# Layer 0 of a four-layer image kernel: all position evictions on VectorE, two images ahead of the other two, and the output maxima spread over the steps

## The chip, the cores and the metric

The kernel runs on one core of one Trainium2 chip. The core has five engines that work side by side, each through its own queue in order: TensorE for matrix products (PE in the profile, with its weight loads shown as PEld), VectorE (DVE), ScalarE (ACT), GpSimd (POOL) and SyncE (SP), which here only issues transfers. They meet through semaphores. Matrix products are written to PSUM, eight banks of 512 float32 columns on 128 partitions; everything else lies in SBUF or in the memory outside the core.

The metric is the device time of one execution in microseconds (us). Lower is better.

## The reference

The input is a float32 tensor of 4 images, 16 channels and 512 x 512 pixels. Four layers follow one another. The change touches the first alone:

```python
pos = conv_general_dilated(x, pos_w, padding=1, feature_group_count=16)   # 3x3 taps, each channel for itself
x = x + pos + pos_b
y = affine(x)                                # per pixel, 16 -> 16 channels
win = windows of 8 x 8 pixels of y           # 64 tokens of 16 channels
q, k, v = win @ qkv_w.T + qkv_b              # 2 heads of 8 channels
attn = softmax(q @ k.T / sqrt(8))            # 64 x 64 in each window and head
x = x + (attn @ v) @ proj_w.T + proj_b
x = x + gelu(affine2(x) @ fc1_w.T + fc1_b) @ fc2_w.T + fc2_b
```

Layer 1 begins with a fake quantisation, for which the largest absolute value of all of layer 0's output must be known: `alpha = max(|x|)`. After it come a 3 x 3 convolution with a batch norm and a clip, a pair of 3 x 3 convolutions with a residual, and a 3 x 3 convolution with a pixelwise MLP.

## The kernel before, in words

Layer 0 is written in `window_attention`. It works in 64 steps. A step n takes a block of 8 rows and 64 columns in eight strips of each of the four images: the 128 partitions hold 4 pairs of strips (V, index `vv`) of 2 x 16 channels, and the images are the index `u`. The loop `for n in range(STEPS)` holds three steps in flight at a time: step n is finished, the keys and queries of step n+1 are made, and the taps of step n+2 are summed.

PSUM is shared out by hand. Banks 0 and 1 are the tile `pair0`, banks 2 and 3 `pair1`; banks 4 to 7 are single. The taps of image u (`depthwise`, L287, nine of them, 32 x 32 matmuls, four for each tap) sum up in bank u. `position` (L302 on VectorE for images 0 and 1, L298 on ScalarE for images 2 and 3) adds the bias and writes them to `y`, in the order of windows. The same four banks later take the scores.

The order on each engine is the order of the program text; nothing reorders it, since the engines stand under `tc.manual_schedule`. A step runs like this:

1. `values(0)` (L338) turns the first values round into bank 4; VectorE copies them out (L346). `scores(0)` (L353) fills banks 0 to 3, four windows of four images; ScalarE takes exponentials of one pair of banks at a time (L361). Then `output` of the step before (L432, L437) adds the second MLP product to the residual, into the tile `xo`.
2. For k = 1 to 7: `scores(k)`, `values(k)` (copied out by ScalarE, at k = 7 by VectorE), `attend(k-1)` (L374), and `divide(k-1)`: two transposes (L389) and a reciprocal (L394) on VectorE, a product on GpSimd (L396), and later `turn_back` (L403) on VectorE. SP issues stores and key turns (L90, L310) here. Each turn ends with one `highest_output()` (L452), which takes the largest absolute value of one piece of `xo`, if the list `largest` holds any.
3. `attend(7)`, the last `divide` and `turn_back`, then 16 blocks of queries and taps, `highest(n + 1)` (L329) on VectorE, one more `highest_output()`, and `project` (L409) with its residual sums (L414).
4. A tail of 44 blocks in an order written as a string. A `d` is one tap of one image; an `h` is one product of the MLP's first layer (`hidden`, L421) with its gelu on ScalarE (L426); a `q` is a query product (L319), copied out by VectorE (L326). Block i works in rows `32 * (i % 4)` of the array, so four blocks that follow one another use different rows. The `h` and `q` blocks take banks 6, 7, 4, 5 in turn.

The tile `xo` covers two steps. Only after the second of them, `store` puts its pieces on the lists `stores` and `largest`, eight maxima of 4 rows by 128 columns. So they are taken in every second step, one at each call of `highest_output()`; these are called even steps below (n even), and the others odd.

In the last step there are no taps and queries, and each image's output is made and sent inside the tail.

Of the kernel before, what the change touches and what calls it, by code (L numbers as in the profile page):

```python
# [12 lines left out]
F32 = mybir.dt.float32  # L13
BF16 = mybir.dt.bfloat16
AF = mybir.ActivationFunctionType
ALU = mybir.AluOpType
# [9 lines left out]
P = 128  # L26
# [5 lines left out]
WS = 8  # L32
# [54 lines left out]
def _store_block(nc, x1, src, b, r0, cols, queues=None):  # L87

    rows = x1.rearrange("m (r c) b x -> (m r) c b x", r=2)[r0 + 1 : r0 + 1 + WS, :, b, cols]
    (next(queues) if queues else nc.sync).dma_start(rows.rearrange("m c x -> c m x"), src)  # L90
# [53 lines left out]
def window_attention(ctx: ExitStack, tc, xw, x1, hots, m, v, peak):  # L144
# [14 lines left out]
    nc = tc.nc  # L159
    U = V = 4  # L160
    BW = 64
    NJ = BW // WS
    N = NJ * T
# [11 lines left out]
    def bank(i):  # L175
        return pairs[i // 2][:, i % 2, :] if i < 4 else singles[i - 4]

    def quad(i):
        return slice(32 * i, 32 * i + 32)
# [3 lines left out]
    def load(k):  # L183
        t = xin.tile([P, V, WS + 2, BW + 2], F32, tag="x", name=f"x{k}")
        nc.sync.dma_start(t, xw[k])
        return t

    xts, ys = {0: load(0), 1: load(1)}, {}
# [72 lines left out]
    px = ctx.enter_context(tc.tile_pool(name="w0x", bufs=2))  # L261
# [15 lines left out]
    def by_window(ap):  # L277
        return ap.rearrange("p (j a x) -> p a j x", a=WS, x=WS)

    def by_row(ap):  # L280
        return ap.rearrange("p (a j x) -> p a j x", a=WS, x=WS)

    def depthwise(n, tap, u):

        dy, dx = divmod(tap, 3)
        for vv in range(V):
            nc.tensor.matmul(  # L287
                bank(u)[quad(vv)], taps[quad(u), tap, :],
                xts[n][quad(u), vv, dy : dy + WS, dx : dx + BW],
                start=tap == 0, stop=tap == 8,  # L290
            )

    def position(n):

        y = px.tile([P, U, N], F32, tag="y", name=f"y{n}", bufs=3)
        for u in range(U):
            if u // 2:
                nc.scalar.activation(  # L298
                    by_window(y[:, u]), by_row(bank(u)), AF.Identity, bias=v("pos_b")
                )  # L300
            else:
                nc.vector.tensor_scalar(  # L302
                    by_window(y[:, u]), by_row(bank(u)), v("pos_b"), None, ALU.add
                )
        return y

    def turn_keys(y, vv):
        for u in range(U):
# [39 lines left out]
    def scores(k, n):  # L348

        vv, jl = k // 2, 4 * (k % 2)  # L350
        for i, jj in ((0, 0), (0, 1), (1, 0), (0, 2), (1, 1), (0, 3), (1, 2), (1, 3)):
            for u in (2 * i, 2 * i + 1):
                nc.tensor.matmul(  # L353
                    bank(u)[:, P * jj : P * jj + P],
                    y2[quad(u), vv, jl + jj].rearrange("p w t -> p (w t)"),
                    g[quad(u), vv, jl + jj].rearrange("p h t -> p (h t)"),
                    start=True, stop=True,
                )
        e = px.tile([P, U, 4, P], F32, tag="e", name=f"e{n}_{k}", bufs=3)
        for i in range(2):  # L360
            nc.scalar.activation(  # L361
                e[:, 2 * i : 2 * i + 2].rearrange("p u j t -> p u (j t)"),
                pairs[i], AF.Exp,
            )
        return e
# [52 lines left out]
    def hidden(y, u, vv, b, n):  # L418

        for k in range(4):  # L420
            nc.tensor.matmul(  # L421
                b[quad(k)], fc1[quad(vv), quad(k)], y[quad(vv), u, :],
                start=True, stop=True,
            )
        hd = px.tile([P, N], F32, tag="hid", name=f"hid{n}_{u}_{vv}", bufs=16)
        nc.scalar.activation(hd, b, AF.Gelu, bias=f1b)  # L426
        return vv, hd

    def output(y, xo, hids, us, banks, n):

        for k, (vv, hd) in enumerate(hids):
            nc.tensor.matmul(  # L432
                bank(banks[k // 4])[quad(vv)], m("fc2"), hd, start=True, stop=True
            )
        at = BW * (n % 2)
        for u, i in zip(us, banks):
            nc.vector.tensor_tensor(  # L437
                xo[:, u, :, at : at + BW].rearrange("p a (j x) -> p a j x", x=WS),
                by_window(bank(i)), by_window(y[:, u]), ALU.add,
            )  # L440
        if n % 2:
            store(xo, n // 2, us)


    queues = itertools.cycle((nc.sync, nc.gpsimd))

    stores, largest = [], []

    def highest_output(k=1):
        for _ in range(min(k, len(largest))):  # L450
            xo, i = largest.pop(0)
            nc.vector.tensor_reduce(  # L452
                peak[:, i : i + 1], xo, AX.XY, ALU.max, apply_absolute_value=True
            )

    def store(xo, k, us):
        i, cb = divmod(k, NQ)
        for u in us:
            for a in range(2):
                half = slice(WS // 2 * a, WS // 2 * a + WS // 2)  # L460
                largest.append((xo[:, u, half], 2 * (U * k + u) + a))
            for strip in range(2 * V):
                stores.append((xo[C * strip : C * strip + C, u], u, SR * strip + WS * i, cb))

    def send(k, queues=None):
        for _ in range(min(k, len(stores))):
            src, u, r, cb = stores.pop(0)
            _store_block(nc, x1, src, u, r, slice(XW * cb, XW * cb + XW), queues)
# [26 lines left out]
    for n in range(2):  # L495
        for tap in range(9):
            for u in range(U):
                depthwise(n, tap, u)
        xts[n + 2] = load(n + 2)
        ys[n] = position(n)  # L500
    highest(0)
    for vv in range(V):
        turn_keys(ys[0], vv)
# [3 lines left out]
    last, xo = None, None  # L507
    nc.scalar.preload_act_table_set("natural_log_exp_and_others")
    for n in range(STEPS):
        more, ahead = n + 1 < STEPS, n + 2 < STEPS  # L510
        taken, asked = [0] * U, [0] * V

        def block(what, i, b, scalar=False):
            at = i % 4
            if what == "q" and more:
                query(ys[n + 1], asked[at], at, b, scalar)
                asked[at] += 1
            elif what == "d" and ahead:
                depthwise(n + 2, taken[at], at)
                taken[at] += 1  # L520
                if taken == [9] * U:
                    ys[n + 2] = position(n + 2)

        values(0)
        es, ts = {0: scores(0, n)}, {}
        if last:

            output(*last)
        for k in range(1, 8):
            es[k] = scores(k, n)  # L530
            values(k)
            attend(es[k - 1], k - 1)
            ts[k - 1] = divide(k - 1, n, nc.gpsimd)
            if 1 < k < 7:
                turn_back(ts[k - 2], k - 2)
            if k == 1:
                send(8 * U)
            if k % 2 and more:
                turn_keys(ys[n + 1], k // 2)
            highest_output()  # L540
        nc.scalar.preload_act_table_set("gelu_and_others")
        attend(es[7], 7)
        ts[7] = divide(7, n, nc.gpsimd)
        for k in (5, 6, 7):
            turn_back(ts[k], k)
        free = iter((4, 5, 6, 7, 4, 5))
        for i, what in enumerate("qqddddqqqqdddddd"):
            block(what, i, bank(next(free)) if what == "q" else None, True)
        if more:
            highest(n + 1)  # L550
        highest_output()
        y = ys.pop(n)
        project(y)
        if n % 2 == 0:
            xo = px.tile([P, U, WS, XW], F32, tag="xo", name=f"xo{n}", bufs=1)
        if not more:
            flag = bounded()

        hids, units = [], itertools.cycle((6, 7, 4, 5))
        for i, what in enumerate("ddddhdhddhqhddhqhddhdhddhdhddhdhdhddhdddddhh"):
            if what == "h":
                q = len(hids)
                hids.append(hidden(y, q // 4, i % 4, bank(next(units)), n))
                if not more and q in (5, 9, 13):
                    u = q // 4 - 1
                    output(y, xo, hids[q - 5 : q - 1], (u,), (u,), n)
                    send(8, queues)
            else:  # L570
                block(what, i, bank(next(units)) if what == "q" else None)
        if n + 4 < STEPS:
            xts[n + 4] = load(n + 4)
        if more:
            nc.scalar.preload_act_table_set("natural_log_exp_and_others")
        last = (y, xo, hids, range(U), (5, 4, 6, 7), n)
    output(y, xo, hids[12:], (3,), (3,), n)
    send(8, queues)
    highest_output(2 * U)
    return nc.values_load(flag[0:1, 0:1], min_val=0, max_val=1)  # L580

# [792 lines left out]
```

## Time and profile before

| | |
|---|---|
| median of 3 runs | 5686.06 us (5681.55 to 5701.97) |
| the profiled execution | 5693.38 us |
| its span, first to last instruction | 5691.6 us |
| mean granted TensorE clock | 0.99 |
| layer 0's 64 steps, first transposes to the end of the loop | about 70 to 3189 us |
| busy in the span: PE, DVE, ACT, POOL | 5428.8, 3738.1, 3482.3, 707.5 us |
| L302 position, VectorE, x128 | 746 ns each |
| L298 position, ScalarE, x128 | 697 ns each |
| L452 maxima, VectorE, x256 | 640 ns each |

The rows of groups in the profile give a line of the code, the engine, the operation, what it writes and reads, how often it runs, its busy time, and the idle time of its engine just before it with what ended that. An engine's idle time matters only where the bottleneck waits for it. A timeline row gives start, duration, engine, line, operation, operands and count; in brackets stands the idle time before it and the releaser. In a list of waits a row gives who waited for whom, the total, how many times, and the longest.

### The profile page before, as it was taken

How to read it: one execution, taken by the hardware profiler on the slowest of the kernel's cores; microseconds unless marked ns; L12 is line 12 of the kernel's file. 1: busy time of each engine (PE TensorE's matmuls, PEld its weight loads, DVE VectorE, ACT ScalarE, POOL GpSimd, SP SyncE). 2: the span in 40 equal slices, each digit the busy share in tenths (PEclk: the TensorE clock that was granted, in tenths of full speed). 3: DMA queues.
4: the chain of work that ended last, by engine and by line, in shares of the span. 5: the costliest groups of instructions: out<-in, count | busy, mean ns of one | idle time of the engine just before them, and what ended most of it. 6: DMA issues, size and time to landing. Idle time of an engine off the chain costs nothing. (4 is left out here: it accounts for less than half of the span.)

```text
span 5691.6 us, 268539 instructions
## 1 busy us (share of the span) xinstructions
PE 5428.8 (95%) x120912; PEld 2891.5 (51%) x120912; DVE 3738.1 (66%) x5806; ACT 3482.3 (61%) x4739; POOL 707.5 (12%) x692
## 2 busy tenths in 40 slices
PE   7999999999999999999999765999999999999999
PEld 5666666666666666666676332322222222222222
DVE  4666666666666666666666555667676767676766
ACT  3777777777777777777777453444444444444444
POOL 1111111111111111111111352000000000000000
PEclk9999999999999999999999898999999999999999
DMA  2333333233333333333323697777767776777674
GB/s 79 77 75 74 77 71 77 65 82 71 80 73 78 73 79 73 74 77 72 81 65 60 140 247 182 173 174 176 175 174 177 174 176 173 177 175 177 173 177 107
DMA packets 626194, 677.47 MB, mean 119 GB/s; under 512 B 355856, under 2 KB 485008, under 8 KB 616848
## 3 DMA queue, kind: packets, MB, share of 16 engines
q1 hardware_dynamic: 624240, 658.76, 48.2%
q8 instruction: 953, 15.61, 1.2%
q14 instruction: 201, 1.65, 0.1%
q0 software_dynamic: 512, 1.05, 0.1%
q10 hardware_dynamic: 288, 0.39, 0.0%
HBM read 222.45 MB, written 134.48 MB: 63 GB/s over the span
## 5 line engine op out<-in xcount | busy, mean ns | idle before, releaser
L361 ACT ACTIVATE e<-pair 128x1024 f32<-128x1024 f32 x1024 | 992.8, 1022 | 449.0 <-PE pair L353 448.1
L287 PE MATMUL pair<-x,taps 32*32 32x512 f32 x18432 | 1073.8, 601 | 3.5 <-issue 2.2
L1206 ACT ACTIVATE hid<-tb,vec 128x512 f32<-128x512 f32 x1024 | 646.8, 684 | 630.7 <-PE tb L1198 630.7
L389 DVE STREAM_TRANSPOSE a<-bank 128x512 f32<-128x512 f32 x1024 | 669.9, 692 | 368.8 <-PE bank L374 354.6
L396 POOL TENSOR_TENSOR t<-a,r 128x512 f32<-128x512 f32 x512 | 542.1, 1059 | 2607.2 <-DVE r L394 2607.2
L426 ACT ACTIVATE hid<-bank,f1b 128x512 f32<-128x512 f32 x1024 | 641.4, 689 | 297.3 <-PE bank L421 233.1
L353 PE MATMUL pair<-g,y 32*128 32x128 f32 x16384 | 727.4, 287 | 50.2 <-DVE y L302 45.2
L1208 DVE TENSOR_SCALAR hid<-tb,vec 128x512 f32<-128x512 f32 x1024 | 717.9, 743 | 27.1 <-PE tb L1198 26.8
L353 PEld LDWEIGHTS pair<-g,y 32*128 32x128 f32 x16384 | 626.2, 186 | 198.1 <-issue 131.8
L421 PE MATMUL bank<-y,fc_e 32*32 32x512 f32 x8192 | 709.2, 606 | 1.0 <-DVE y L414 1.0
L374 PE MATMUL bank<-e,yt 64*32 64x128 f32 x32768 | 608.2, 274 | 28.1 <-DVE yt L346 21.0
L287 PEld LDWEIGHTS pair<-x,taps 32*32 32x32 f32 x18432 | 502.0, 103 | 182.2 <-issue 67.9
L1198 PE MATMUL tb<-ye,mat 32*128 32x512 f32 x4096 | 586.1, 639 | 0.0
L374 PEld LDWEIGHTS bank<-e,yt 64*32 64x32 f32 x32768 | 463.3, 106 | 128.3 <-issue 105.0
L1218 PE MATMUL tb<-hid,mat 128*32 128x512 f32 x4096 | 466.0, 595 | 0.0
L1123 PE MATMUL tb<-zo,cw 64*32 64x512 f32 x3096 | 365.7, 598 | 16.1 <-issue 8.9
L1123 PE MATMUL tb<-xo,cw 64*32 64x512 f32 x3096 | 361.5, 594 | 7.2 <-issue 5.3
L302 DVE TENSOR_SCALAR y<-pair,vec 128x512 f32<-128x512 f32 x128 | 90.2, 746 | 413.2 <-PE pair L287 413.2
L1123 PE MATMUL tb<-ho,cw 64*32 64x512 f32 x3072 | 357.4, 592 | 3.8 <-issue 3.0
L1123 PE MATMUL tb<-ze,cw 64*32 64x512 f32 x3072 | 360.8, 598 | 0.0
L1123 PE MATMUL tb<-he,cw 64*32 64x512 f32 x3072 | 357.7, 592 | 0.0
L1123 PE MATMUL tb<-xe,cw 64*32 64x512 f32 x3072 | 357.0, 594 | 0.0
(180 smaller groups left out, 7044.3 us busy)
## 6 DMA issues: line engine op xcount, KB each, us to landing
x<-in_xw_dram SPq DMA_DIRECT2D x64, 1320.0 KB, 5.8
zo<-ze SPq DMA_DIRECT2D x512, 128.5 KB, 2.4
ho<-he SPq DMA_DIRECT2D x512, 128.5 KB, 2.4
xo<-xe SPq DMA_DIRECT2D x512, 128.5 KB, 2.4
y<-y SPq DMA_DIRECT2D x2048, 32.0 KB, 2.6
tx<-x SPq DMA_DIRECT2D x256, 256.0 KB, 4.1
out_dram<-xe SPq DMA_DIRECT2D x128, 512.0 KB, 4.6
x<-xo SPq DMA_DIRECT2D x1008, 64.0 KB, 2.6
```

What stands on the lines that cost most here:

```text
L287: nc.tensor.matmul(bank(u)[quad(vv)], taps[quad(u), tap, :], xts[n][quad(u), vv, dy : dy + WS, dx : dx + BW], start=tap == 0, stop=tap == 8,)
L353: nc.tensor.matmul(bank(u)[:, P * jj : P * jj + P], y2[quad(u), vv, jl + jj].rearrange("p w t -> p (w t)"), g[quad(u), vv, jl + jj].rearra ...
L361: nc.scalar.activation(e[:, 2 * i : 2 * i + 2].rearrange("p u j t -> p u (j t)"), pairs[i], AF.Exp,)
L374: nc.tensor.matmul(bank(4 + 2 * (k % 2) + w)[quad(u), P * jj : P * jj + P], t[half, U * jj + u, w : w + 2].rearrange("p d c -> p (d c)"), ...
L389: nc.vector.transpose(a[:, 512 * w : 512 * w + 512], bank(4 + 2 * (k % 2) + w))
L396: engine.tensor_tensor(t.rearrange("p b w c -> p w b c"), top, r.unsqueeze(3).to_broadcast([P, 2, 16, C]), ALU.mult,)
L421: nc.tensor.matmul(b[quad(k)], fc1[quad(vv), quad(k)], y[quad(vv), u, :], start=True, stop=True,)
L426: nc.scalar.activation(hd, b, AF.Gelu, bias=f1b)
L1123: nc.tensor.matmul(p[r][_quad(2 * f + w)], weights[_half(r), odd, dx, :], src[_half(r), f, dx : dx + W], start=dx == 0, stop=dx == 2,)
L1198: nc.tensor.matmul(p[q], w1[_quad(q), 1 - par, :], inner(src)[_quad(q), f, :], start=True, stop=True,)
L1206: nc.scalar.activation(hd, p[q], AF.Relu, bias=v("l3_b1"))
L1208: nc.vector.tensor_scalar(hd, p[q], v("l3_b1"), 0.0, ALU.add, ALU.max)
```

## The change

All four images' positions are now written by VectorE. `position(n, i)` does one pair of images, and is called as soon as the nine taps of that pair are in: images 2 and 3 (`pair1`) come first, then 0 and 1. `scores` goes through the pairs in the other order, `pair1` first, and its exponentials too. The string of the tail is another one: the taps of images 2 and 3 are complete at places 34 and 35 (counted from 0), those of images 0 and 1 at 40 and 41 as before; two query blocks stand side by side; and `h` blocks no longer run image by image, each row of the array counts its own images. In the last step an output is made when the next `h` belongs to a later image and the four of that image are there.

The maxima are taken for each step by itself: four pieces of 8 rows by 64 columns, put on the list in `output`, and taken at k = 1 to 4. The calls at k = 5 to 7 and behind `highest(n + 1)` are gone.

```diff
-    def position(n):
-
-        y = px.tile([P, U, N], F32, tag="y", name=f"y{n}", bufs=3)
-        for u in range(U):
-            if u // 2:
-                nc.scalar.activation(
-                    by_window(y[:, u]), by_row(bank(u)), AF.Identity, bias=v("pos_b")
-                )
-            else:
-                nc.vector.tensor_scalar(
-                    by_window(y[:, u]), by_row(bank(u)), v("pos_b"), None, ALU.add
-                )
-        return y
+    def position(n, i):
+
+        if n not in ys:
+            ys[n] = px.tile([P, U, N], F32, tag="y", name=f"y{n}", bufs=3)
+        for u in (2 * i, 2 * i + 1):
+            nc.vector.tensor_scalar(
+                by_window(ys[n][:, u]), by_row(bank(u)), v("pos_b"), None, ALU.add
+            )
...
-        for i, jj in ((0, 0), (0, 1), (1, 0), (0, 2), (1, 1), (0, 3), (1, 2), (1, 3)):
+        for i, jj in ((1, 0), (1, 1), (0, 0), (1, 2), (0, 1), (1, 3), (0, 2), (0, 3)):
...
-        for i in range(2):
+        for i in (1, 0):
             nc.scalar.activation(
...
         at = BW * (n % 2)
+        for u in us:
+            largest.append((xo[:, u, :, at : at + BW], 2 * (U * (n // 2) + u) + n % 2))
...
-            for a in range(2):
-                half = slice(WS // 2 * a, WS // 2 * a + WS // 2)
-                largest.append((xo[:, u, half], 2 * (U * k + u) + a))
...
-        ys[n] = position(n)
+        for i in range(2):
+            position(n, i)
...
-                if taken == [9] * U:
-                    ys[n + 2] = position(n + 2)
+                if at % 2 and taken[at - 1 : at + 1] == [9, 9]:
+                    position(n + 2, at // 2)
...
-            highest_output()
+            if k < 5:
+                highest_output()
...
         if more:
             highest(n + 1)
-        highest_output()
...
-        hids, units = [], itertools.cycle((6, 7, 4, 5))
-        for i, what in enumerate("ddddhdhddhqhddhqhddhdhddhdhddhdhdhddhdddddhh"):
+        hids, units, sent = [[] for _ in range(U)], itertools.cycle((6, 7, 4, 5)), 0
+        used = [0] * U
+        for i, what in enumerate("ddddhdhddhqqhddhdhddhdhddhddhddhdhddddhhddhh"):
             if what == "h":
-                q = len(hids)
-                hids.append(hidden(y, q // 4, i % 4, bank(next(units)), n))
-                if not more and q in (5, 9, 13):
-                    u = q // 4 - 1
-                    output(y, xo, hids[q - 5 : q - 1], (u,), (u,), n)
+                at = i % 4
+                u = used[at]
+                used[at] += 1
+                if not more and sent < u and len(hids[sent]) == U:
+                    output(y, xo, hids[sent], (sent,), (sent,), n)
                     send(8, queues)
+                    sent += 1
+                hids[u].append(hidden(y, u, at, bank(next(units)), n))
...
-    output(y, xo, hids[12:], (3,), (3,), n)
-    send(8, queues)
+    for u in range(sent, U):
+        output(y, xo, hids[u], (u,), (u,), n)
+        send(8, queues)
     highest_output(2 * U)
```

## The prediction

> **What bounds the kernel now.** I read the page first, then the PE's waits, then one step's timeline engine by engine, then the distance from step to step.
>
> ```profile
> PE 5428.8 (95%) x120912; PEld 2891.5 (51%) x120912; DVE 3738.1 (66%) x5806; ACT 3482.3 (61%) x4739; POOL 707.5 (12%) x692
> ```
>
> ```profile
> PE tb L1048 <- ACT qe L1014: 90.6, 125, 2.3
> PE pair L353 <- DVE y L302: 45.2, 62, 0.7
> PE bank L374 <- DVE yt L346: 21.0, 45, 1.1
> ```
>
> TensorE is the engine to shorten. Only the last two waits lie in layer 0, and both are on VectorE: 62 times the scores of a new step wait for a position eviction, 45 times an attend waits for the value copy. The page's chain covers only the time after 3521 us, so it says nothing of layer 0.
>
> A step is counted from its first value transposes (L338). In the timeline 63 such distances average 48.62 us: 49.24 after an even step, 47.97 after an odd one. The difference of 1.27 us is the eight maxima (L452), which all fall into even steps. The first fence is VectorE in an even step (it began at 1528.06), the second in an odd step (began at 1383.00).
>
> ```profile
> 1554.29 0.66 DVE L403 STREAM_TRANSPOSE o<-t 128x512 f32<-128x512 f32 x1
> 1554.86 0.64 DVE L452 TENSOR_REDUCE peak<-xo 128x1 f32<-128x512 f32 x1
> 1555.43 0.68 DVE L346 COPY yt<-bank 128x512 f32<-128x512 f32 x1
> ...
> 1557.63 0.63 DVE L452 TENSOR_REDUCE peak<-xo 128x1 f32<-128x512 f32 x1
> ...
> 1563.89 0.67 DVE L452 TENSOR_REDUCE peak<-xo 128x1 f32<-128x512 f32 x1
> 1564.48 2.06 DVE L414 SCALAR_TENSOR_TENSOR y<-bank,pb,y 128x512 f32<-128x512 f32 x3
> ```
>
> ```profile
> 1409.24 0.65 DVE L403 STREAM_TRANSPOSE o<-t 128x512 f32<-128x512 f32 x1
> 1409.82 0.65 DVE L346 COPY yt<-bank 128x512 f32<-128x512 f32 x1
> ...
> 1418.67 2.07 DVE L414 SCALAR_TENSOR_TENSOR y<-bank,pb,y 128x512 f32<-128x512 f32 x3 [0.81 <-issue]
> ```
>
> In the even step a maximum stands between the transpose and the value copy that attend(7) needs; two more stand in the serial run of VectorE up to the residual sums (L414). Median start of attend(7): 28.28 us into an even step, 27.61 into an odd one, where the last exponential is what ends the wait. Median first L414: 36.74 against 35.53; in the odd step VectorE even stands idle 0.81 us before it, so there its own queue is no longer the limit.
>
> The step's end, PE, then VectorE, then ScalarE:
>
> ```profile
> 1527.37 0.76 PE L421 MATMUL bank<-y,fc_e 32*32 32x512 f32 x8
> 1528.06 0.66 PE L338 MATMUL bank<-mat,y 128*128 128x128 f32 x4
> 1529.44 1.27 PE L353 MATMUL pair<-g,y 32*128 32x128 f32 x32 [0.73 <-DVE y L302]
> ```
>
> ```profile
> 1527.97 1.41 DVE L302 TENSOR_SCALAR y<-pair,vec 128x512 f32<-128x512 f32 x2 [6.35 <-PE pair L287]
> ```
>
> ```profile
> 1527.10 1.28 ACT L298 ACTIVATE y<-pair,vec 128x512 f32<-128x512 f32 x2
> 1528.26 1.28 ACT L426 ACTIVATE hid<-bank,f1b 128x512 f32<-128x512 f32 x2
> 1529.56 1.28 ACT L575 ACT_TABLE_LOAD   x1
> ```
>
> Scores start when the second eviction of images 0 and 1 ends (1529.38), 0.73 us after the transposes.
>
> **The change, part by part.**
>
> *Maxima.* Same 256 instructions of 512 elements a lane. They leave k=5, 6, 7 and the place behind L329, and stand at k=1 to 4 of every step. In before, even steps carry them there too, and PE reaches the transposes of k=5 only 0.13 us later than in odd steps (mean 19.73 against 19.60): a turn of VectorE with one maximum is 1.31+0.35+0.65+0.64 less overlaps, about 2.87, and PE's turn is 3.05. Should PE's turn fall below 2.87 this cover is gone. The new shape is 8 rows of 64 instead of 4 rows of 128; L437 writes that shape at the duration of other 512-element rows (692 ns), so I keep 0.64; bounds 0.60 and 0.70. So even steps come down to odd ones plus 0.1: 49.24-48.07 = 1.17, times 32 = -37. Odd steps take up 0.1: 31 x 0.1 = +3.
>
> *Evictions.* 128 ScalarE rows of 697 ns become VectorE rows of 746 ns. Back to back one follows the other after 0.67 (ScalarE: 0.58). In the tail VectorE stood idle 6.35 us before L302. The taps of images 2 and 3 now end at places 34 and 35 of the 44 blocks (counted from 0), those of 0 and 1 still at 40 and 41; six blocks at 0.28 are 1.7 us, just over the 1.34 us that the first two evictions need. So the second pair starts where it did. The scores now begin with images 2 and 3: two of their eight groups (8 of 32 records, 0.3 of 1.2 us) run inside today's 0.73 us wait, then PE waits for images 0 and 1 as before. Ceiling 0.3 a step, not 0.73. Floor -0.2, if VectorE enters the second pair late. I take 0.2: 62 x 0.2 = -12. Reversing the exponentials only mirrors the two pairs.
>
> [...]
>
> *ScalarE relieved.* It loses 2 x 0.58 = 1.16 us in the tail. I count this at nothing: there PE is the limit. Depthwise alone, with nothing to wait for, runs like this in the prologue:
>
> ```profile
> 43.00:53.20 10.20, 9.64 (x288) 5.33 (x288) 1.00 0.31 124
> ```
>
> 288 records are 36 blocks of eight, about 0.28 us each. The tail has 44 blocks in about 12.5 us, 0.28 again. And ScalarE still ends with two gelus of H3 (last two blocks, both versions), then the table load: exp(0) starts about 2.8 us into the step as now, and scores(1), behind the 3.6 us of the fc2 matmuls (L432), doesn't wait for it.
>
> *New order of blocks.* Bank 4, which the next step's transposes overwrite, was last used by the gelu unit at place 33, now at 38 (H2.2). A block at place 42 starts 1.14 us before the transposes, so place 38 starts about 2.0 before; a gelu starts 1.1 after its block and takes 0.69: it ends about 0.2 us before it is needed. Cost 0, between -0.2 (the early wait for a VectorE key eviction, L326, is gone) and +0.6 (one gelu late). Behind that wait are all of PE's next step; nothing else moves: SP and POOL issue the same DMAs in the same order, and SP's stores (19.9 us) plus key turns (25.6) still fit into two steps.
>
> *Prologue.* PE waited 1.22 us there until VectorE and ScalarE had emptied the first positions (43.07). Four in a row on VectorE: +1.2 for the first, +1.3 in front of L329 and the key evictions for the second: +2.5.
>
> *Last step.* Images are finished later: each output now waits for the gelu just issued. ScalarE's gaps there were 0.73+1.84+1.00+1.00 = 4.6 us; three of about 2.2 are 6.6: +2. Half of the last eight maxima (4.83 us) leave, but SP's issues end at 3193.1 and must land, so 0.
>
> Sum: -37 + 3 - 12 + 2.5 + 2 = -41.5. The profiled execution took 5693.4 (span 5691.6), so 5652 on its scale. It lies 0.13% above the median of the runs, 5686.1; on that scale 5644.
>
> **The rivals.**
>
> (a) Forecast: 5620 to 5670. 0.62.
>
> (b) The freed ScalarE shortens the tail. For: PE's tail has waits on gelus and key evictions at places 10 to 16. Against: 0.28 a block overall. At 0.5 us a step, 31 us more: 5613. 0.12.
>
> (c) The maxima's cost is only spread: each step, not each second, is 0.6 late, because at k=1 to 4 VectorE falls behind and doesn't recover. For: a turn has only 0.18 us of slack. Against: without maxima at k=5 and 6 it regains about 0.8 a turn. Then only 12 less 4.5 are won: 5678. 0.14.
>
> (d) Slower. The transposes of the next step wait in bank 4 for the gelu of H2.2. One gelu (0.58) late costs 62 x 0.58 = 36 and eats the gain; it decides the sign from 0.67 us a step. Two late (1.16) give 5644+72 = 5716. For: place 38, only 0.2 us in hand, and ScalarE runs close behind PE. Against: it has 1.16 us less to do. 0.12.
>
> **How the numbers follow.** A change of 0.5% (28 us) is about what a measurement of this kernel can tell from none. Of (a) about nine tenths lie beyond it; with (b) that makes 0.68 faster. The rest of (a) and (c) give 0.20 same; (d) 0.12. The range runs from the middle of (b), 5605, to beyond (c), 5685; it leaves out (d) and the far end of (b).
>
> **What would show it.** Right: even and odd steps equal, near 47.9; L353's wait for the positions below 0.5 us and after 8 records, not before the first; attend(7) near 27.6 in all steps; tail still about 12.5. Wrong: a wait of L338 for a gelu at the step's start (d); L389 late at k=2 to 4 (c); gelus closer together and a tail under 12 us (b).

## The result and the profile after

The changed kernel takes 5649.66 us (median of 8 runs, 5636.82 to 5661.27), the one before 5686.48 (median of 8, 5664.99 to 5701.97): ratio 0.9939, 95% interval 0.9923 to 0.9955, so faster by 0.6%. A second set on another occasion gave 0.9938 (0.9924 to 0.9951). The forecast was 5644. The profiled execution took 5653.74 (span 5651.9), where the working had 5652 on the profile's scale.

The page's first line, and its row of the position evictions (busy us, mean ns | idle before):

```profile
PE 5441.0 (96%) x120912; PEld 2960.7 (52%) x120912; DVE 3826.3 (68%) x5934; ACT 3427.9 (61%) x4610; POOL 707.4 (13%) x692
L298 DVE TENSOR_SCALAR y<-pair,vec 128x512 f32<-128x512 f32 x256 | 180.3, 747 | 349.8 <-PE pair L287 349.8
```

256 evictions now stand on VectorE, each at 747 ns. The maxima take 639 ns in their new shape (640 before), and the other groups of the loop keep their mean durations within 1%. PE's waits (us in total, times, longest):

```profile
PE tb L1047 <- ACT qe L1013: 91.1, 124, 1.8
...
PE bank L369 <- ACT e L356: 12.8, 44, 0.3
```

Both layer-0 waits on VectorE are off the head of this list: 45.2 us of the scores on the positions, 21.0 us of attend on the value copy. What is left of attend's wait (line 369) is on the exponential or, by the profile, on nothing that it shows.

The start of a step on PE (transposes 333, scores 348, fc2 427):

```profile
1071.54 0.83 PE L416 MATMUL bank<-y,fc_e 32*32 32x512 f32 x8
1072.30 0.66 PE L333 MATMUL bank<-mat,y 128*128 128x128 f32 x4
1072.88 1.86 PE L348 MATMUL pair<-g,y 32*128 32x128 f32 x32
1074.68 2.35 PE L427 MATMUL bank<-hid,mat 128*32 128x512 f32 x20
```

and the same moment on VectorE:

```profile
1070.39 1.41 DVE L298 TENSOR_SCALAR y<-pair,vec 128x512 f32<-128x512 f32 x2 [5.05 <-PE pair L287]
1072.12 1.41 DVE L298 TENSOR_SCALAR y<-pair,vec 128x512 f32<-128x512 f32 x2 [0.32 <-PE pair L287]
```

The first pair ends 0.5 us before the transposes begin, the second 1.23 us after they began (1.32 in the step of before that the prediction shows). The scores start at once, on images 2 and 3, and stretch from 1.2-1.3 us to 1.86.

VectorE late in an even step (one that began at 1120.19):

```profile
1146.14 0.65 DVE L398 STREAM_TRANSPOSE o<-t 128x512 f32<-128x512 f32 x1
1146.72 0.65 DVE L341 COPY yt<-bank 128x512 f32<-128x512 f32 x1
...
1152.72 2.25 DVE L324 TENSOR_REDUCE most<-y 128x1 f32<-128x2048 f32 x1
1156.38 2.07 DVE L409 SCALAR_TENSOR_TENSOR y<-bank,pb,y 128x512 f32<-128x512 f32 x3 [1.42 <-issue]
```

No maximum stands between transpose and value copy any more, and VectorE is idle before the residual sums (1.42 us here, 0.41 in the median of the even steps). Even steps average 47.96 us now, odd ones 47.71 (before 49.20 and 47.98). Averages of even and odd steps leave out the first two distances and the last one of the 63, here and below.

The whole span by sections. A "step" is the distance between the first value transposes of two steps; the last step runs from its transposes to the first matmul of layer 1. "Again" is a second profile of the changed kernel.

| us | before | after | after again | foreseen change |
|---|---|---|---|---|
| up to the first step | 70.06 | 72.14 | 71.69 | +2.5 |
| 63 steps, mean | 48.615 | 47.846 | 48.020 | -46 in all |
| last step | 72.07 | 79.68 | 75.71 | +2 |
| layer 1 | 2486.7 | 2485.9 | 2485.6 | 0 |
| span | 5691.6 | 5651.9 | 5658.3 | -41.5 |

Two profiles of one program differ by 0.17 us a step, 11 us over the loop; smaller differences of the mean step are not read in what follows. A ratio with an interval stands behind each experiment; it compares with the kernel before on the same chip. The chips are not alike: on that of e1, e2, e3 and e7 the kernel before took 5674.88 (median of 53), 11.6 us less than above, and it was not profiled there. So the mean steps of these four, set against the table, hold an unknown part of 11.6 us, up to 0.18 a step, that is the chip's. Where steps and ratios disagree, the ratios decide.

### The profile page after: what moved, and what is told of

It reads as the page before. It is cut to its first block, busy times and chain, and to the rows that moved or that the text cites. A ratio compares the mean times of both kernels' runs of the same rounds, so it can differ in the third digit from the quotient of the medians.

```text
span 5651.9 us, 268227 instructions
## 1 busy us (share of the span) xinstructions
PE 5441.0 (96%) x120912; PEld 2960.7 (52%) x120912; DVE 3826.3 (68%) x5934; ACT 3427.9 (61%) x4610; POOL 707.4 (13%) x692
## 5 line engine op out<-in xcount | busy, mean ns | idle before, releaser
L287 PE MATMUL pair<-x,taps 32*32 32x512 f32 x18432 | 1043.2, 603 | 4.2 <-issue 2.4
L421 ACT ACTIVATE hid<-bank,f1b 128x512 f32<-128x512 f32 x1024 | 653.5, 687 | 332.7 <-PE bank L416 245.7
L348 PE MATMUL pair<-g,y 32*128 32x128 f32 x16384 | 757.7, 286 | 3.7 <-issue 2.0
L348 PEld LDWEIGHTS pair<-g,y 32*128 32x128 f32 x16384 | 650.5, 186 | 153.5 <-issue 136.6
L416 PE MATMUL bank<-y,fc_e 32*32 32x512 f32 x8192 | 722.3, 610 | 0.6 <-DVE y L409 0.4
L287 PEld LDWEIGHTS pair<-x,taps 32*32 32x32 f32 x18432 | 531.3, 103 | 164.6 <-issue 54.8
L298 DVE TENSOR_SCALAR y<-pair,vec 128x512 f32<-128x512 f32 x256 | 180.3, 747 | 349.8 <-PE pair L287 349.8
L1197 PEld LDWEIGHTS tb<-ye,mat 32*128 32x128 f32 x4096 | 162.8, 183 | 377.5 <-issue 370.4
```

The costliest lines, as they stand in the source:

```text
L287: nc.tensor.matmul(bank(u)[quad(vv)], taps[quad(u), tap, :], xts[n][quad(u), vv, dy : dy + WS, dx : dx + BW], start=tap == 0, stop=tap == 8,)
L348: nc.tensor.matmul(bank(u)[:, P * jj : P * jj + P], y2[quad(u), vv, jl + jj].rearrange("p w t -> p (w t)"), g[quad(u), vv, jl + jj].rearra ...
L416: nc.tensor.matmul(b[quad(k)], fc1[quad(vv), quad(k)], y[quad(vv), u, :], start=True, stop=True,)
L1197: nc.tensor.matmul(p[q], w1[_quad(q), 1 - par, :], inner(src)[_quad(q), f, :], start=True, stop=True,)
```

## The two parts alone

**e1_maxima_only** is the kernel before with the new order of maxima alone:

```diff
+        for u in us:
+            largest.append((xo[:, u, :, at : at + BW], 2 * (U * (n // 2) + u) + n % 2))
...
-            highest_output()
+            if k < 5:
+                highest_output()
...
         if more:
             highest(n + 1)
-        highest_output()
```

**e2_evictions_only** is the changed kernel with the maxima as in the kernel before.

> The kernel before, with only the maxima changed: four of 8x64 a step, at k = 1 to 4. Theory (the place of the maxima is what costs; 49.20 us for an even step, 47.98 for an odd one in before): even steps fall by 1.1 to 1.2, odd ones rise by 0 to 0.1, attend(7) starts near 27.6 in both, the scores' wait for the positions stays at 0.73. Mean step 48.0 to 48.1 against 48.62, so 32 to 38 us less in all; prologue and last step unchanged. Rival (the cost is only spread over all steps): mean step stays at 48.6, the time is that of before within 5 us.

> The changed kernel with the maxima as before (eight of 4x128 in every second step). Theory: even and odd steps stay 1.2 apart, both 0.2 to 0.3 below before (49.0 and 47.7), because only a quarter of the scores moves into the wait: 13 to 19 us less in the 63 steps. Against it stand the prologue (+2) and the last step (+7.6, both measured in the changed kernel), so the time is 4 to 9 us below before, hardly to be told from it. Rival (evictions and order make most of the gain): steps 0.7 lower, 35 us less.

Measured: e1 0.9955 (0.9941 to 0.9968), mean step 48.07, even 48.17 and odd 47.93. e2 0.9979 (0.9966 to 0.9991), mean step 48.22, even 48.71 and odd 47.65. PE's waits of e1:

```profile
PE pair L353 <- DVE y L302: 45.2, 62, 0.7
PE bank L374 <- DVE yt L346: 8.1, 37, 0.2
```

and of e2:

```profile
PE bank L369 <- DVE yt L341: 18.4, 27, 0.8
```

Each part takes away its own wait: e1 keeps the scores' wait whole and has 8.1 of 21.0 us left at attend, e2 keeps 18.4 at attend and has no wait of the scores on the positions on its list.

By the ratios the maxima alone bring 0.45%, 26 us (18 to 33), and the evictions alone 0.21%, 12 us (5 to 19). Together that is 0.66%, against 0.61% (0.45 to 0.77) of the whole change: the two add up, as far as the intervals tell. The profiles give more for each part, 0.546 x 63 = 34 us for the maxima, and for the evictions 0.395 x 63 = 25 in the loop less 2.1 in the prologue and 5.1 in the last step. But these are steps of one chip set against steps of another, and the two surpluses, 8 and 6 us, are no larger than the 11.6 us by which the kernel before differs between the chips.

## Which place of a maximum costs

**e7_maxima_late** is the changed kernel with the four maxima at k = 4 to 7:

```diff
-            if k < 5:
+            if k > 3:
                 highest_output()
```

**e12_one_behind_highest** leaves three at k = 1 to 3 and puts the fourth behind the maximum of the positions:

```diff
-            if k < 5:
+            if k < 4:
                 highest_output()
...
         if more:
             highest(n + 1)
+        highest_output()
```

> The changed kernel, but the four maxima of each step stand at k = 4 to 7 instead of 1 to 4. Theory (place, not number): the maximum of k = 6 stands before the value copy of k = 7 again, and that of k = 7 in the serial run before the residual sums, so every step starts attend(7) 0.5 to 0.6 later (near 28.1) and is 0.8 to 1.0 longer: mean step 48.6 to 48.8 against 47.85, so 50 to 60 us above the changed kernel. Rival (balance, four a step instead of eight in every second, is what helps): within 10 us of the changed kernel.

> The changed kernel with the maxima at k = 1, 2, 3 and the fourth behind the reduction of y (L329), where before had one too. Theory (moving them late to k = 4 to 7 cost only 0.13 to 0.29 us a step, so the larger part of before's 1.2 must be this place, in front of the residual sums that the first hidden blocks wait for): the sums start 0.4 to 0.6 later, attend(7) stays near 27.5; mean step 0.3 to 0.6 longer, 20 to 38 us above the changed kernel. Rival (the sums wait for PE anyway, and before's cost comes from attend(7) alone): within 8 us of the changed kernel.

Measured: e7 0.9987 (0.9976 to 0.9997), mean step 48.14, even and odd alike (48.19, 48.12). e12 0.995 (0.9934 to 0.9965), mean step 48.00, where the two profiles of the changed kernel have 47.85 and 48.02. On the same chip the changed kernel has 0.9938 (0.9924 to 0.9951): the medians are 8 us apart, which the intervals do not separate. PE's waits, of e7:

```profile
PE bank L369 <- DVE yt L341: 41.3, 58, 1.1
```

and of e12:

```profile
PE bank L369 <- ACT e L356: 12.3, 43, 0.5
```

In e7 attend(7) does start late, 27.97 us into the even steps (median) instead of 27.5, and the wait is there 58 times. But 0.8 to 1.0 a step was expected, and the profiles show only 0.1 to 0.3. By the ratios e7 is 0.5% above the changed kernel: 28 us, or 0.4 a step, about the delay of attend(7). VectorE's idle time before the first residual sum (median, us) says why it is not more:

| | even | odd | late maxima, even / odd |
|---|---|---|---|
| before | 0.00 | 0.35 | two / none |
| after | 0.41 | 0.36 | none |
| e1 | 0.52 | 0.33 | none |
| e12 | 0.00 | 0.00 | one (behind the maximum of the positions) |
| e7 | 0.02 | 0.01 | one (k = 7) |

"Late" is k = 7 or behind the maximum of the positions. Both lie in VectorE's run to the sums, behind the value copy that attend(7) needs, and share one slack of 0.3 to 0.5 us (0.63 and 0.51 in the second profile of the changed kernel). One maximum of 0.64 just about uses it up and costs nothing that is clear of the noise (e12). Two, 1.28, should pass it by some 0.8 to 0.9, and the even steps of the kernel before had two; this is an estimate, for no run has two late maxima without a late attend(7) as well. In the kernel before the sums start 1.21 us later in even steps than in odd ones, of which attend(7) has 0.67. The expectation for e7 gave each step the price of such an even step; with one late maximum only the delay at attend(7), 0.45, is left.

Spreading alone brings little: an even and an odd step together take 96.36 us in e2 (48.71 + 47.65) and 96.31 in e7 (48.19 + 48.12), both on one chip, and the ratios (0.9979, 0.9987) do not set them apart. What pays is to be in front of the stretch in which VectorE is the last to be ready: 95.67 in the changed kernel (47.96 + 47.71; 95.96 in its second profile), with ratios of 0.9939 and 0.9938.

## What hides the evictions: the order, not the engine

Five kernels vary how the positions are emptied. **e3_four_in_a_row** is the kernel before with all four evictions on VectorE, at the old place and in the old order:

```diff
         for u in range(U):
-            if u // 2:
-                nc.scalar.activation(
-                    by_window(y[:, u]), by_row(bank(u)), AF.Identity, bias=v("pos_b")
-                )
-            else:
-                nc.vector.tensor_scalar(
-                    by_window(y[:, u]), by_row(bank(u)), v("pos_b"), None, ALU.add
-                )
+            nc.vector.tensor_scalar(
+                by_window(y[:, u]), by_row(bank(u)), v("pos_b"), None, ALU.add
+            )
```

**e8_old_order** is the changed kernel with the tail's old string, so that the first pair is complete two blocks before the second and not six:

```diff
-        for i, what in enumerate("ddddhdhddhqqhddhdhddhdhddhddhddhdhddddhhddhh"):
+        for i, what in enumerate("ddddhdhddhqhddhqhddhdhddhdhddhdhdhddhdddddhh"):
```

**e9_scalar_first_pair** is the changed kernel with images 2 and 3 on ScalarE again:

```diff
-            nc.vector.tensor_scalar(
-                by_window(ys[n][:, u]), by_row(bank(u)), v("pos_b"), None, ALU.add
-            )
+            if u // 2:
+                nc.scalar.activation(
+                    by_window(ys[n][:, u]), by_row(bank(u)), AF.Identity, bias=v("pos_b")
+                )
+            else:
+                nc.vector.tensor_scalar(
+                    by_window(ys[n][:, u]), by_row(bank(u)), v("pos_b"), None, ALU.add
+                )
```

> The kernel before, with images 2 and 3 evicted by VectorE too, at the same place (images 0 to 3 in a row once all taps are in), nothing else changed. [...] Theory: images 2 and 3 are ready 1.34 us later than 0 and 1; the scores begin with images 0 and 1 at 1.39 us into the step as now, then stall at their fifth record until 2.75; the scores end near 3.6 instead of 2.6, and the value copy of k = 0 is 1.3 later. The gelus end 1.16 earlier on ScalarE, which nobody waits for. So 0.9 to 1.2 us a step, 55 to 75 us slower than before. Rival (a freed ScalarE gives it back in the tail): within 20 us of before.

> The changed kernel with the old string of the tail (taps of images 2 and 3 end at places 38 and 39, right before those of 0 and 1 at 40 and 41). Theory (the six blocks between the pairs are what hides the first pair's evictions): VectorE gets to images 0 and 1 about 0.7 us later, so the scores stall until about 2.05 us into the step and end 0.6 to 0.8 later: 30 to 50 us above the changed kernel in the steps, less 0 to 7 in the last step. Rival (the order of the string matters only to PE's own packing): within 12 us.

> The changed kernel with images 2 and 3, whose taps end first, evicted by ScalarE as in before. Theory (the tail is bound by PE, and the freed ScalarE is worth nothing; what counts is that the pair is done early): steps within 0.15 of 47.85, the last gelus and exp(0) 1.2 us later; the prologue 2 us shorter. Within 10 us of the changed kernel. Rival b (the freed 1.16 us of ScalarE is part of the gain): steps longer by 0.3 to 0.6, 20 to 38 us above the changed kernel.

Measured: e8 1.0025 (1.0011 to 1.0039), mean step 48.56: 0.55 to 0.7 us a step more than the changed kernel. VectorE in one step of e8, then its PE wait:

```profile
1044.63 2.73 DVE L298 TENSOR_SCALAR y<-pair,vec 128x512 f32<-128x512 f32 x4 [5.48 <-PE pair L287]
```

```profile
PE pair L348 <- DVE y L298: 33.0, 62, 0.5
```

Four in a row last 2.73 us, and the scores wait for the last two. e9, on the same chip, gave 0.9943 (0.9921 to 0.9965) and a mean step of 47.97, the same as the changed kernel, with the first pair on ScalarE. What pays is that the first pair is complete six blocks before the second; which engine then empties it makes no difference that shows. In e9 the next step's transposes began 0.64 us after the last hidden record started (median; 0.57 to 0.78) instead of 0.52: the gelu of the block on bank 4 ended only 0.05 before them, where in the changed kernel it ended 0.35 before. That is rival (d), at about 0.12 us.

e3 gave 1.0253 (1.0225 to 1.0281), +146 us against the 5674.88 of the kernel before on its chip. PE at the start of one step:

```profile
1286.28 0.66 PE L333 MATMUL bank<-mat,y 128*128 128x128 f32 x4
1287.67 0.71 PE L348 MATMUL pair<-g,y 32*128 32x128 f32 x8 [0.74 <-DVE y L297]
1288.99 1.16 PE L348 MATMUL pair<-g,y 32*128 32x128 f32 x24 [0.60 <-DVE y L297]
1290.08 5.34 PE L427 MATMUL bank<-hid,mat 128*32 128x512 f32 x32
```

and three windows of the same step (window, length, busy time of PE, PEld, DVE, ACT, POOL with instructions, granted clock, DMA share, GB/s):

```profile
1286.28:1290.00 3.72, 2.38 (x40) 1.91 (x36) 3.25 (x5) 2.71 (x4) 0.00 (x0) 1.00 0.74 267
1290.00:1293.60 3.60, 3.60 (x24) 0.99 (x24) 0.69 (x1) 1.77 (x2) 0.00 (x0) 0.53 0.26 104
1293.60:1298.00 4.40, 4.40 (x118) 2.67 (x111) 2.08 (x3) 1.39 (x2) 0.00 (x0) 1.00 0.73 131
```

PE stalls twice, 0.74 and 0.60 us, and then the granted TensorE clock is at 0.5 for 3.4 us: each group of four fc2 matmuls comes about 0.85 us after the last instead of 0.43, and 32 of them take 5.34 us, where the kernel before has 3.64. This happened in 53 of the 63 steps, which average 51.30 us. The 10 without it average 49.50: the bare price of the stall is 0.9 a step (as expected; 62 x 0.9 = 56 us, well under half of the loss), the clock's is 1.8 more.

Which steps are hit can be read from the trace. In the whole of e3 every stretch of half clock begins on one grid of 3.413 us; in the kernel before and in the changed kernel too the beginnings lie whole multiples of 3.413 us apart, and one stretch of the changed kernel, from 3075.62 to 3092.68 us, lasts five times that. In the loop, each of the 53 that start there follows a grid window in which PE was busy for no more than 66% of the time, and none follows the other 888 windows, in which PE was busy for 71% or more. The ten steps that escape are those in which a line of the grid falls 1.0 to 2.35 us into the step and so divides the stalls between two windows. First the window before the drop above, then two windows next to each other in a step that escaped:

```profile
1286.77:1290.19 3.42, 2.08 (x38) 1.61 (x40) 2.76 (x5) 2.45 (x4) 0.00 (x0) 1.00 0.88 321
884.00:887.42 3.42, 3.08 (x79) 1.67 (x60) 1.08 (x2) 2.57 (x5) 0.00 (x0) 1.00 0.13 26
887.42:890.83 3.41, 2.42 (x40) 1.78 (x44) 2.25 (x4) 2.44 (x3) 0.00 (x0) 1.00 0.92 353
```

PE was not idle in the window before the drop: it was busy in 2.08 of 3.42 us.

**e11_row_covered** was to tell stall and clock apart: e3 with the fc2 products of images 0 and 1 put ahead of the scores, as work to lie over the evictions.

```diff
         values(0)
+        if last:
+            yl, xl, hl, _, bl, nl = last
+            output(yl, xl, hl[: 4 * 2], range(2), bl[:2], nl)
         es, ts = {0: scores(0, n)}, {}
         if last:
-            output(*last)
+            output(yl, xl, hl[4 * 2 :], range(2, U), bl[2:], nl)
```

> The kernel with four evictions in a row on VectorE at the step's end (2.5% slower than before, its granted TensorE clock at half for about 3 us at nearly every step's start), with the fc2 products of images 0 and 1 moved ahead of scores(0). Theory (PE standing idle there trips the clock, and the row itself is cheap when PE has work): scores(0) starts at 2.3, its stall is below 0.4, the clock stays at 1.00 in the steps, mean step 48.3 to 48.8: 150 us or so below the uncovered row, about the time of before. Rival (the longer run of VectorE itself delays the later work): mean step stays above 50.

Measured: 1.014 (1.0124 to 1.0155), mean step 49.79. The clock stayed at 1.00, but the cover failed:

```profile
1265.77 1.06 PE L427 MATMUL bank<-hid,mat 128*32 128x512 f32 x8
1268.47 1.07 PE L427 MATMUL bank<-hid,mat 128*32 128x512 f32 x8 [1.64 <-DVE yt L341]
1269.47 1.27 PE L348 MATMUL pair<-g,y 32*128 32x128 f32 x32
```

```profile
1265.18:1269.00 3.82, 2.18 (x24) 0.74 (x20) 3.82 (x6) 2.55 (x3) 0.00 (x0) 1.00 0.74 264
```

The product of image 1 goes to bank 4, which holds the value transposes until VectorE's copy, and that copy stands behind the four evictions. PE stands still 1.64 us in one piece, and in this window it is busy no more (2.18 of 3.82) than in e3's (2.38 of 3.72), yet the clock holds. On e11's own grid 48 windows of the loop have PE busy for 65% or less, down to 51%, and none is followed by a drop. And in the changed kernel the clock falls to 0.5 at 3075.62 us, late in the loop, right after a grid window in which PE was busy throughout, with 32 x 32 matmuls:

```profile
3072.20:3075.62 3.42, 3.42 (x56) 0.71 (x47) 2.81 (x5) 1.40 (x3) 0.00 (x0) 1.00 0.19 35
```

So the busy share parts the windows within e3, but it is not what decides. The windows differ in the work that fills them: mostly scores (32 rows, 128 columns) in e3, fc2 products (128 rows, 512 columns) in e11. No run varies that alone, and what exactly lowers the clock stays open.

**e4_split_last_pair** gives image 1, one of the pair that ends last, to ScalarE, so that two engines empty that pair.

```diff
-            nc.vector.tensor_scalar(
-                by_window(ys[n][:, u]), by_row(bank(u)), v("pos_b"), None, ALU.add
-            )
+            if u == 1:
+                nc.scalar.activation(
+                    by_window(ys[n][:, u]), by_row(bank(u)), AF.Identity, bias=v("pos_b")
+                )
+            else:
+                nc.vector.tensor_scalar(
+                    by_window(ys[n][:, u]), by_row(bank(u)), v("pos_b"), None, ALU.add
+                )
```

> The changed kernel, but image 1 is evicted by ScalarE (between the gelus of H2.3 and H3.2), so that the two evictions that fall together at the step's end run on two engines. Theory: the pair is ready 0.8 us into the step instead of 1.33; the scores' stall after eight records goes, they end 0.4 to 0.5 earlier. ScalarE's last gelus, its table load and exp(0) come 0.58 later (3.4 instead of 2.8), still ahead of scores(1) near 5.4. So 0.25 to 0.5 us a step, 15 to 30 us below the changed kernel. Rival (exp(0) or the wait for the last exponential takes it back): steps within 0.1 of 47.85.

Measured: 0.9955 (0.9942 to 0.9968), mean step 48.12; no gain. VectorE, then ScalarE in one step:

```profile
1085.06 0.75 DVE L303 TENSOR_SCALAR y<-pair,vec 128x512 f32<-128x512 f32 x1 [0.33 <-PE pair L287]
```

```profile
1085.84 0.69 ACT L299 ACTIVATE y<-pair,vec 128x512 f32<-128x512 f32 x1 [0.36 <-DVE y L303]
1089.00 1.94 ACT L361 ACTIVATE e<-pair 128x1024 f32<-128x1024 f32 x2
```

ScalarE began 0.03 us after VectorE had ended, and the profile names VectorE's eviction as what it waited for, all 64 times (62.5 us in total). Both images lie in one PSUM tile of a pair, in different banks, and in one tile y. That y is shared cannot be the reason by itself: in the kernel before two engines write one y side by side, from two pairs, for 0.41 us in the median of the 64 steps. That the wait goes with the pair's tile is the author's guess; no run gives each bank a tile of its own. The pair was ready 1.27 us into the step, as without the split, and ScalarE's exponentials of scores(0) began at 3.75 instead of 2.69.

## The last step, and a version that beats both

**e5_last_step_old** is the changed kernel whose last step alone uses the old string and makes outputs as the kernel before did. **e10_one_output_first** is e5 with the fc2 product of image 0, whose bank is free by then, put ahead of the scores in every step. First a piece of what e5 changes (its old order of outputs is not printed here), then what e10 adds:

```diff
-        for i, what in enumerate("ddddhdhddhqqhddhdhddhdhddhddhddhdhddddhhddhh"):
+        order = "ddddhdhddhqqhddhdhddhdhddhddhddhdhddddhhddhh" if more else "ddddhdhddhqhddhqhddhdhddhdhddhdhdhddhdddddhh"
+        for i, what in enumerate(order):
...
```

```diff
         values(0)
+        if last:
+            yl, xl, hl, _, bl, nl = last
+            output(yl, xl, hl[: 4 * 1], range(1), bl[:1], nl)
         es, ts = {0: scores(0, n)}, {}
         if last:
-            output(*last)
+            output(yl, xl, hl[4 * 1 :], range(1, U), bl[1:], nl)
```

**e13_changed_again** is the changed kernel itself, on the chip of e10.

> The changed kernel with the last step alone written as before (old string, outputs after the 6th, 10th and 14th hidden block). Theory: the changed kernel loses 7.6 us between the start of the last step and the first matmul of layer 1 (79.7 against 72.1) because each output waits for the gelu just issued; this gives 6.5 to 8 of them back, the steps stay at 47.85. Rival (the loss comes from the first transfers of layer 1, or from the maxima at the end): no more than 2 us back.

> The changed kernel with the last step as before, and the fc2 product of image 0 of the previous step moved ahead of scores(0), so that PE has 0.86 us of work while VectorE empties the last two images. Theory: scores(0) starts 1.45 us into the step with both pairs ready (1.3), runs without its stall and ends near 2.65; three products remain, so scores(1) starts near 5.4 instead of 5.86; exp(0) keeps its start at 2.7 to 2.8, behind the table load. 0.3 to 0.45 us a step, 20 to 28 us, and about 5 us in the last step: 25 to 33 us below the changed kernel of this call. Rival (the gain goes again before attend(7), where the exponentials set the pace): steps within 0.15 of the changed kernel's, only the last step's 5 us remain.

> The changed kernel itself, for a comparison on the same chip, and for the spread between two profiles of one program. Expected: 0.994 of before; mean step between 47.8 and 48.1; first step to last as in its first profile within 10 us; the stretch from the last step to layer 1 between 73 and 80 us.

Measured: e5 0.9944 (0.9928 to 0.9961), last step 72.87 us against 79.68 and 75.71; 3 to 7 us are too little to show in the ratio. All seven profiles with the new string in the last step have 73.5 to 79.7, the six with the old one, the kernel before and e8 among them, 70.1 to 72.9; e10, also with the old one, has 68.96. ScalarE in the last step of the changed kernel:

```profile
3127.96 2.01 ACT L421 ACTIVATE hid<-bank,f1b 128x512 f32<-128x512 f32 x3 [10.49 <-PE bank L416]
3131.36 1.35 ACT L421 ACTIVATE hid<-bank,f1b 128x512 f32<-128x512 f32 x2 [1.39 <-PE bank L416]
3136.60 2.42 ACT L421 ACTIVATE hid<-bank,f1b 128x512 f32<-128x512 f32 x4 [3.89 <-PE bank L416]
3139.34 1.27 ACT L421 ACTIVATE hid<-bank,f1b 128x512 f32<-128x512 f32 x2 [0.31 <-PE bank L416]
3144.30 1.84 ACT L421 ACTIVATE hid<-bank,f1b 128x512 f32<-128x512 f32 x3 [3.69 <-PE bank L416]
3148.30 1.27 ACT L421 ACTIVATE hid<-bank,f1b 128x512 f32<-128x512 f32 x2 [2.16 <-PE bank L416]
```

Between the first and the last gelu its gaps are 1.39 + 3.89 + 0.31 + 3.69 + 2.16 = 11.4 us. In e5 they are 4.8, in the second profile of the changed kernel 9.6. PE's windows over the same stretch, from the first fc1 matmul to the last fc2, first of the changed kernel, then of e5:

```profile
3125.97:3150.67 24.70, 24.16 (x160) 4.03 (x160) 4.92 (x11) 10.15 (x16) 7.40 (x14) 0.64 0.27 54
```

```profile
3136.00:3153.90 17.90, 17.90 (x160) 3.60 (x160) 4.92 (x11) 10.03 (x16) 7.40 (x14) 0.78 0.39 77
```

6.8 us more for the same 160 matmuls, at a mean granted clock of 0.64 instead of 0.78. The second profile of the changed kernel has 22.70 us at 0.76: at nearly e5's clock the new order still takes 4.8 us longer, as much as its gaps are longer (9.6 against 4.8). So most of the loss is the order's, and the spread between the two profiles goes with the clock.

e10: 0.9892 (0.9877 to 0.9908), 5624.3 us, against 0.9938 (0.9924 to 0.9951) and 5654.67 of the changed kernel on the same chip: 30 us less time. The start of one of its steps:

```profile
1068.91 0.66 PE L333 MATMUL bank<-mat,y 128*128 128x128 f32 x4
1069.50 1.07 PE L427 MATMUL bank<-hid,mat 128*32 128x512 f32 x8
1070.50 1.27 PE L348 MATMUL pair<-g,y 32*128 32x128 f32 x32
1071.70 2.78 PE L427 MATMUL bank<-hid,mat 128*32 128x512 f32 x24
```

One product, 1.07 us long, lies over the second pair's eviction, and the scores run through without a gap, 1.27 instead of 1.86. scores(1) starts 5.50 us into the step instead of 5.85, and the mean step is 47.52, 0.3 to 0.5 less than in three profiles of the unchanged loop (47.85, 48.01, and 48.02 on the same chip). The rest is the last step's. This is what stayed of the wait at the positions; unlike image 1 in e11, image 0 has a bank that no copy holds.

## Why the prediction was right

*Maxima.* The step stands: 34 us were foreseen; alone (e1) they bring 26 (18 to 33) by the ratio and 34 by the profile, which compares two chips, and on top of the evictions 23 by the ratios of e2 and the changed kernel (13 to 24 by the profiles). attend(7) came as foreseen (28.28 before, 27.51 now, in even steps), and even and odd steps meet near 47.9 (47.96 and 47.71; 48.11 and 47.84 in the second profile). The odd steps do not show the 0.1 for what they took up. What the working did not have is the slack in the run to the sums: one late maximum is about free there (e12), and by VectorE's idle time it is the second one that pays. Rival (c), a cost that is only spread, is what e7 shows for late places; for k = 1 to 4 it is out.

*Evictions in the loop.* 0.2 a step was taken between -0.2 and 0.3. The ratio of e2 gives 12 us in all; with the 7 us lost in its prologue and last step that is some 0.3 a step, and e1 against the changed kernel gives 0.05 to 0.22 by the profiles. As foreseen, the scores start on the first pair and meet the old wait after 8 records; from the eighth to the ninth it is 0.16 us in the median (0.07 where nothing is waited for), and the 0.73 before the first are gone. The last score record comes at 2.09 instead of 2.39, scores(1) 0.30 earlier. Only 0.15 of it reaches attend(7) in odd steps, where the exponential sets the pace.

*Four in a row.* e3 and e8 show when four evictions cost: where they fall together, in e3 146 us (some 56 for the stall, the rest with the fallen clock), in e8 0.55 to 0.7 us a step; with the pairs six blocks apart they don't, the first pair on either engine (0.9939, and 0.9943 in e9).

*ScalarE relieved: nothing.* Confirmed twice: PE's stretch from the last projection to the end of the last hidden block is 12.18 us, in e1, where ScalarE still has its evictions, 12.25 (medians; before 12.25 in odd steps and 12.78 in even ones), and e9, which gives the two evictions back to ScalarE, has 12.17 and takes the same time. Rival (b) is out.

*New order, bank 4: nothing.* In the changed kernel the gelu ends 0.35 us before the transposes (0.2 foreseen), and they start as long after the last hidden record as before, 0.52. Rival (d) exists, at 0.12 us, only when ScalarE has the evictions as well (e9).

*Prologue.* +2.5 foreseen, +2.1 measured, +1.6 in the second profile.

*Last step.* This term failed in its size: +2 foreseen, +7.6 measured (+3.6 again). "Three of about 2.2" were ScalarE's gaps in the working; they are 3.89, 3.69 and 2.16, with 1.39 and 0.31 besides, and the granted clock was not in the sum at all. On the profile's scale the total came within 2 us of the forecast because the loop brought 2.5 us more than foreseen, layer 1 0.8 and the prologue 0.4, against 5.6 us less from the last step; in the second profile the loop brought 8.5 less. By the medians of the runs the change brings 36.8 us where 42 were foreseen; the last step's excess is of that size, but the interval of the ratio (26 to 44 us) does not tell 36.8 from 42. That the total came so near is in part luck: the last step cost 2 to 6 us more than foreseen, and the ratios give less for the maxima (26 where 34 were foreseen) and more for the evictions, prologue and last step included (12 where 7.5 were), each within its interval or near it.

## What to carry to other kernels

A row of evictions was hidden here by the distance between the pieces of work that they wait for, more than by sharing it over engines: let one half become ready several blocks earlier, begin the consumer with that half, and put a piece of ready work with a free bank before the half that is late. Work that can stand anywhere belongs in front of the stretch in which its engine is the last to be ready; spreading it inside that stretch brought little. A short stall is to be costed with what it may do to the clock: in e3 0.9 us a step became 2.7.

## What the runs showed of the hardware that was not expected

Stalls of 0.74 and 0.60 us with 8 matmuls between them were followed by half the granted clock for 3.4 us, in 53 of 63 steps of e3, and trebled their price (0.9 to 2.7 us a step). In e3, in the kernel before and in the changed kernel the drops start whole multiples of 3.413 us apart, and in e3 it is the busy share of PE in one grid window that parts the steps that are hit (66% or less) from those that escape (71% or more). One idle stretch of 1.64 us in e11 was not followed by a drop, though its grid windows are busy for as little as 51%; and a window of the changed kernel that was busy throughout, with 32 x 32 matmuls, was. Two engines that read two banks of one PSUM tile ran one after the other, the second starting 0.03 us after the first had ended (e4); in the kernel before, on different pairs, they overlapped by 0.41 us (median of the 64 steps).
